# Self-attention key and value projections as seven quarter products in one go, with token sums on GpSimd and weight sums formed once

## The chip, the cores and the metric

The kernel runs on one core of a Trainium2 chip. The metric is the device time of one execution in microseconds (us). Engines: PE is TensorE (matmuls and transposes; its weight loads stand as PEld), DVE is VectorE, ACT is ScalarE, POOL is GpSimd, SP issues the DMAs.

## The reference

An encoder layer over a context of 77 tokens and a decoder layer over 2048 tokens, for two batches, width 512, 16 heads of 32, all in fp32. The part that matters is the decoder's causal self-attention:

```python
yn = _ln(y, dec_n1_s, dec_n1_b)
y = y + _mha(yn, yn, dec_sa_in_w, dec_sa_in_b, dec_sa_out_w, dec_sa_out_b, sb)
# in _mha, with xq = xkv = yn:
wq, wk, wv = jnp.split(w_in, 3, axis=0)
q = (xq @ wq.T + bq) ...;  k = (xkv @ wk.T + bk) ...;  v = (xkv @ wv.T + bv) ...
scores = jnp.einsum("bhqd,bhkd->bhqk", q, k) / sqrt(hd) + bias
attn = jax.nn.softmax(scores, axis=-1)
out = jnp.einsum("bhqk,bhkd->bhqd", attn, v)
```

After it come cross attention over the encoder's output and a feed-forward layer of width 2048.

## The kernel before

**Blocks and units.** The self-attention works through 8 blocks of 512 tokens, `(b, m)` for two batches and m = 0 to 3. A block has 16 units, one for each group of four heads (g) and each tile of 128 query tokens (t), so there are 128 units; u is the number of a block's first unit, x the block's number from 0. Because of the causal mask, a unit has m*4 + t + 1 chunks of 128 keys (1 to 16).

**What a unit does.** PE forms the scores of four heads (`scores`, L373), up to four chunks to a bank of PSUM. DVE copies them to SBUF and takes the maxima (L382, L389), then their negative maximum `nm` (L399). ACT forms four exponentials over the whole row, one per head (L404). PE transposes the probabilities (`turn`, L427), chunk by chunk with the four heads of each; half of the transposed tiles are copied from PSUM by ACT (L433) and half by DVE (L431). PE then multiplies by the values (`values`, L444). PSUM has 7 banks in a ring (`bank()`), taken by scores, transposes and projections alike.

**The order of the work** is fixed by hand. All engines' queues are filled by one program loop: transposes of up to eight chunks of unit n, then (after the last of them) `slot(n + 1)`, then the next scores, then the values of unit n, then more scores. A slot holds jobs written into dictionaries by slot number: `light` (ahead of the projections), `jobs` (projections) and `late`:

```python
def slot(n):
    for f in light[n]:
        f()
    for _, run, _ in jobs[n]:
        load_next()
        run(loaded[ran[0]])
        ran[0] += 1
    for f in late[n]:
        f()
```

Up to two of the later exponentials of unit n + 1 are queued on ACT during the transposes of unit n, the rest behind `slot(n + 1)`.

**Projections.** Each of `q_job` (L216), `k_job` (L227), `v_job` (L240) and `out_job` (L252) is four matmuls of 128x512 into one bank and one drain. Queries and keys are made by group of heads (weights of 256 KB into `wqk`, L200), values and outputs by tile of 128 tokens (weights of 1 MB into the one buffer `wbig`, L206). The drain of the keys is on ACT for m < 2 (L232) and on DVE otherwise (L230), that of the values on DVE (L243). The 16 jobs of a block lie in 16 slots, from u-5 to u+10: query u-5, u-1, u+3, u+5; keys u-4, u, u+4, u+6; values u-3, u-2, u+1, u+2 (for m = 0: u+1 to u+4; one slot later for the second block); outputs u+7 to u+10. So nearly each slot has one job. The first slots of all also have the encoder's stages (L544 to L634), and slots 65 to 94 a first part of the cross attention.

**GpSimd in the self-attention** has the power of the variance (L286), the norm's centring (L293), residual sums (L267), the division of the outputs (L472), the encoder's subtraction and division (L596, L608), and from the third block on differences of the feed-forward weights (line L1113).

**The seven products.** The feed-forward layer and the later cross attention already use Winograd's form for a product of 2x2 quarters: seven products (table `ONE`) with sums of quarters of the weights (S1 to S4) and of the tokens (T1 to T4), in place of eight. There a product of 128x256 matmuls runs at L1376, L1493 and L1536. The sums of weights are made once on GpSimd during the self-attention (`wc_sums`) and stored in DRAM.

Of the kernel before, what the change touches and what calls it, by code (L numbers as in the profile page):

```python
# [10 lines left out]
F32 = mybir.dt.float32  # L11
AF = mybir.ActivationFunctionType
ALU = mybir.AluOpType
# [41 lines left out]
def tile_encoder_decoder(ctx: ExitStack, tc: tile.TileContext, ins, out):  # L55
    nc = tc.nc
    x, src = ins["x"], ins["ctx_1024"]
# [8 lines left out]
    dram = ctx.enter_context(tc.tile_pool(name="dram", bufs=1, space=DRAM))  # L66
# [11 lines left out]
    def vec(name, i):  # L78
        c = _COL[name] + i
        return vecs[:, c : c + 1]  # L80
# [78 lines left out]
    with (  # L159
# [6 lines left out]
        kT = ac.tile([P, NC, T], F32, name="kT")  # L166
        vv = ac.tile([P, T // P, D], F32, name="vv")
# [27 lines left out]
        nTs, qTs, ots, sums_of = {}, {}, {}, {}  # L195
        wbig, xs, xr = {}, {}, {}
# [26 lines left out]
        def k_job(b, m, g):  # L223
            def run(w):
                mm = bank()
                for c in range(NC):
                    nc.tensor.matmul(mm, w[:, c, :], nTs[b, m][:, c, :], start=(c == 0), stop=(c == NC - 1))  # L227
                d, bi = kT[:, g, ts(m, MB)], vec("dec_sa_in_b", NC + g)
                if m >= 2:
                    nc.vector.tensor_scalar(d, mm, bi, None, ALU.add)  # L230
                else:
                    nc.scalar.activation(d, mm, AF.Identity, bias=bi)  # L232

            return lambda: small_w(D + g * P), run, True

        def v_job(b, m, t):
            def run(w):
                mm = bank()
                for c in range(NC):
                    nc.tensor.matmul(  # L240
                        mm, nTs[b, m][:, c, ts(t, P)], w[:, c, :], start=(c == 0), stop=(c == NC - 1)
                    )
# [168 lines left out]
        got = {}  # L411
# [515 lines left out]
            return plan  # L927


        blocks = [(b, m) for b in range(B) for m in range(NMB)]  # L930
        NU = NC * TB
        jobs = {n: [] for n in range(-1, len(units) + NU)}
        light = {n: [] for n in range(-1, len(units) + NU)}

        ahead = {n: [] for n in range(-1, len(units) + NU)}
        late = {n: [] for n in light}

        for x, (b, m) in enumerate(blocks):
            u = x * NU
            first = m == 0  # L940

            jobs[max(u - 5, -1)].append(q_job(b, m, 0))
# [52 lines left out]
        v = pp[:H, 13056 : 13056 + 3 * LT].rearrange("h (m u) -> h m u", u=LT)  # L995
# [96 lines left out]
        light[len(units) - 1].append(last_loads)  # L1092


        TOK = MB // 2
        gp, ve = nc.gpsimd, nc.vector


        w1_d = dram.tile([4, NC, P, D], F32, name="w1_d")
# [3 lines left out]
        free = pp[:, 3 * HC * MB : END - 3 * HC * MB]  # L1103
# [8 lines left out]
        def minus(engine, out, a, b):  # L1112
            engine.tensor_tensor(out, a, b, ALU.subtract)  # L1113

        def w2_sums(c):

# [49 lines left out]
        def quarter(name, r, c):  # L1166

            return ins[name][r * TOK : (r + 1) * TOK, c * TOK : (c + 1) * TOK].rearrange("(c p) o -> p c o", p=P)

        def wc_sums(name, turned):  # L1170
            z = free.rearrange("p (z k o) -> p z k o", z=8, k=2)
            q = {}
            for i, (r, c) in enumerate(((0, 0), (0, 1), (1, 0), (1, 1))):
                nc.sync.dma_start(z[:, i], quarter(name, c, r) if turned else quarter(name, r, c))
                q[r, c] = z[:, i]
            s1, s2, s3, s4 = (z[:, 4 + i] for i in range(4))
            if turned:
                gp.tensor_tensor(s1, q[1, 0], q[1, 1], ALU.add)
                minus(gp, s2, s1, q[0, 0])
                minus(gp, s3, q[0, 0], q[1, 0])  # L1180
                minus(gp, s4, q[0, 1], s2)
            else:
                minus(gp, s1, q[0, 1], q[0, 0])
                minus(gp, s3, q[1, 1], q[0, 1])
                minus(gp, s2, q[1, 1], s1)
                minus(gp, s4, q[1, 0], s2)

        def wc_store(dst):
            nc.sync.dma_start(
                dst.rearrange("s p x -> p s x"), free[:, 4 * D :].rearrange("p (s x) -> p s x", s=4)  # L1190
            )

        for u, name, turned, dst in (
            (2 * NU, "dec_ca_in_wT", True, wq_d), (6 * NU, "dec_ca_out_wT", False, wo_d)
        ):
            light[u + 7].append(lambda name=name, turned=turned: wc_sums(name, turned))
            late[u + 8].append(lambda dst=dst: wc_store(dst))
# [6 lines left out]
        u = 6 * NU  # L1204
        for n, k in enumerate((0, 2, 4, 10)):
# [5 lines left out]

        ONE = (
            ("11", "11", 0, True, "11"),
            ("12", "21", 1, True, "11"),
            ("S2", "T2", 0, False, "12"),
            ("S1", "T1", 1, True, "22"),
            ("S3", "T3", 0, False, "22"),
            ("S4", "22", 1, False, "12"),  # L1220
            ("22", "T4", 0, False, "21"),
        )
        TWO = (
            ("11", "11", 0, True, "11"),
            ("S1", "T1", 1, True, "22"),
# [67 lines left out]
        def of_n(name):  # L1293
# [5 lines left out]
        T_OF = {"T1": ("12", "11"), "T2": ("22", "T1"), "T3": ("22", "12"), "T4": ("21", "T2")}  # L1299

        def sum_n(name, of):
            minus(gp, of(name), *(of(a) for a in T_OF[name]))


        sets = [[high[:, (4 * a + k) * D : (4 * a + k + 1) * D] for k in range(4)] for a in range(2)]
# [59 lines left out]
        chains = [None]  # L1365
# [243 lines left out]
        i = 0  # L1609
        while i < len(stream):  # L1610
            n = stream[i][0]
# [91 lines left out]
```

## Time and profile before

| | |
|---|---|
| median of 3 runs | 2808.68 us (2805.91 to 2808.88) |
| profiled execution | 2804.72 us, span 2802.9 us |
| mean granted clock of TensorE | 0.995 |
| DMA | 355 MB, mean 127 GB/s |
| self-attention | from 28 us (first transposes of unit 0) to about 1726 us |

Groups stand as: line, engine, operation, out<-in, shape, count | busy us, mean ns of one | idle time before them and what ended it. Timelines stand as: start us, length us, engine, line, operation, operands, count [idle before <-releaser]. Matmuls are pipelined, so the length of one in a group mean is longer than its share of the busy time.

### The profile page before, as it was taken

The page shows a single profiled execution, that of the slowest core. Times are in us where ns is not written, and L with a number is a line of the kernel's source. Part 1 is how long each engine was busy: PE and PEld are TensorE (multiplying, and loading weights), DVE is VectorE, ACT ScalarE, POOL GpSimd, SP SyncE. Part 2 cuts the span into 40 slices and gives each one's busy share as a digit, 9 for nine tenths or more (in the row PEclk, how much of TensorE's full clock was granted, in tenths as well). Part 3 has the DMA queues.
Part 4 walks back from the last instruction along what each step waited for, and adds up shares of the span by engine and source line. Part 5 has one row for each costly group of instructions (what it writes and reads, how often), then busy time and mean ns, then how long its engine had stood idle before and what let it go on. Part 6 is the DMA issues. An engine that isn't in the chain of part 4 may idle for free. (4 is left out here: it accounts for less than half of the span.)

```text
span 2802.9 us, 65879 instructions
## 1 busy us (share of the span) xinstructions
PE 2769.8 (99%) x25998; PEld 2079.2 (74%) x25998; DVE 1858.9 (66%) x5360; ACT 1430.6 (51%) x2751; POOL 875.4 (31%) x745
## 2 busy tenths in 40 slices
PE   9899999999999999999999999999999999999998
PEld 5557666666666556666666677898989898989898
DVE  4666587778887567687778886464555655464645
ACT  3544466556666546656656676435343444444431
POOL 0301043300100302221200001374647474746456
PEclk9899999999999999999999999999999999999999
DMA  6414344411112512232310113574747574656475
GB/s 174 128 45 138 121 144 125 133 37 40 39 40 77 137 53 62 92 107 88 104 40 17 41 57 130 167 245 143 240 146 244 170 228 161 224 162 222 145 228 181
DMA packets 281270, 355.30 MB, mean 127 GB/s; under 512 B 37968, under 2 KB 156544, under 8 KB 280834
## 3 DMA queue, kind: packets, MB, share of 16 engines
q1 hardware_dynamic: 280962, 351.10, 40.3%
q8 instruction: 205, 3.36, 0.5%
q14 instruction: 103, 0.84, 0.1%
HBM read 309.51 MB, written 41.49 MB: 125 GB/s over the span
## 5 line engine op out<-in xcount | busy, mean ns | idle before, releaser
L404 ACT ACTIVATE pp<-pp,nm 128x128 f32<-128x128 f32 (+15 forms) x512 | 612.1, 1202 | 231.8 <-DVE nm L399 231.4
L382 DVE TENSOR_SCALAR_CACHE_REDUCE pp<-psum 128x512 f32<-128x512 f32 (+3 forms) x1024 | 559.4, 590 | 65.2 <-PE psum L373 63.4
L427 PEld LDWEIGHTS psum<-ident,pp 128*128 128x128 f32 x4352 | 472.4, 141 | 106.0 <-DVE pp L382 51.9
L427 PE MATMUL psum<-ident,pp 128*128 128x128 f32 x4352 | 533.2, 277 | 7.0 <-ACT pp L404 3.7
L433 ACT COPY pts<-psum 128x512 f32<-128x512 f32 (+3 forms) x592 | 297.0, 575 | 435.2 <-PE psum L427 305.4
L431 DVE COPY pts<-psum 128x512 f32<-128x512 f32 (+2 forms) x544 | 330.0, 659 | 66.0 <-PE psum L427 65.7
L373 PE MATMUL psum<-kT,q 32*128 32x512 f32 (+3 forms) x2560 | 357.1, 575 | 4.9 <-DVE pp L382 2.5
L444 PEld LDWEIGHTS psum<-pts,vv 128*32 128x32 f32 x8704 | 226.0, 110 | 124.4 <-issue 116.6
L1405 PE MATMUL psum<-pp 128*128 128x128 f32 x2560 | 304.5, 276 | 1.9 <-POOL pp L1113 1.6
L1405 PEld LDWEIGHTS psum<-pp 128*128 128x128 f32 x2560 | 296.3, 192 | 8.6 <-issue 2.8
L444 PE MATMUL psum<-pts,vv 128*32 128x128 f32 x8704 | 279.0, 275 | 0.7 <-ACT pts L433 0.5
L1113 POOL TENSOR_TENSOR pp<-pp 128x512 f32<-128x512 f32 x159 | 212.6, 1354 | 108.7 <-DMA pp<-in_dec_ff_wT_dram 49.7
L1376 PE MATMUL psum<-vv,pp 128*128 128x256 f32 x1024 | 236.2, 381 | 0.0
L373 PEld LDWEIGHTS psum<-kT,q 32*128 32x128 f32 x2560 | 123.8, 184 | 140.2 <-issue 91.3
L1376 PEld LDWEIGHTS psum<-vv,pp 128*128 128x128 f32 x1024 | 190.3, 190 | 25.8 <-issue 0.5
L389 DVE CUSTOM_DVE_ANT_0 pp<-psum,bias 128x256 f32<-128x256 f32 (+1 forms) x512 | 195.9, 411 | 16.7 <-PE psum L373 16.6
L1389 DVE TENSOR_TENSOR kT<-kT,psum 128x512 f32<-128x512 f32 x96 | 65.8, 686 | 190.0 <-PE psum L1376 189.8
L1376 PE MATMUL psum<-nT,pp 128*128 128x256 f32 x768 | 174.1, 380 | 0.0
L1392 ACT ACTIVATE kT<-kT,vecs 128x256 f32<-128x256 f32 x192 | 87.0, 501 | 156.7 <-DVE kT L1389 156.0
L286 POOL TENSOR_TENSOR rstd<-rstd,mhalf 128x1 f32<-128x1 f32 x32 | 18.5, 578 | 472.4 <-DVE rstd L285 450.9
L1376 PEld LDWEIGHTS psum<-nT,pp 128*128 128x128 f32 x768 | 144.2, 190 | 20.3 <-issue 1.6
L472 POOL TENSOR_TENSOR oT<-rirows,oT 128x512 f32<-128x512 f32 x30 | 38.6, 1287 | 357.3 <-DMA rirows<-rec 270.5
(207 smaller groups left out, 3792.7 us busy)
## 6 DMA issues: line engine op xcount, KB each, us to landing
pp<-w_d SPq DMA_DIRECT2D x520, 256.0 KB
pp<-in_dec_ff_wT_dram SPq DMA_DIRECT2D x112, 256.0 KB
wqk<-in_dec_sa_in_wT_dram SPq DMA_DIRECT2D x64, 256.0 KB
bias<-tzg SPq DMA_DIRECT2D x128, 128.0 KB
pp<-wo_d SPq DMA_DIRECT2D x56, 256.0 KB
wbig<-in_dec_sa_in_wT_dram SPq DMA_DIRECT2D x8, 1024.0 KB
vv<-in_enc_ff_wT_dram SPq DMA_DIRECT2D x8, 1024.0 KB
wbig<-in_dec_sa_out_wT_dram SPq DMA_DIRECT2D x8, 1024.0 KB
```

The source lines that it names most:

```text
L373: nc.tensor.matmul(banks[r][:, : kn * P], q[rows4(r), ts(t, P)], kT[rows4(r), g, k0 * P : (k0 + kn) * P], start=True, stop=True,)
L382: nc.vector.tensor_scalar(p[:, k0 * P : (k0 + far) * P], s[:, : far * P], 1.0, None, ALU.mult, ALU.max, accum_out=st["mx"][:, r, c : c + 1],)
L389: nc.vector.tensor_tensor_reduce(p[:, (i + 1) * P - w : (i + 1) * P], s[:, far * P : kn * P], biases[b, m, g][:, r, 2 * P - w :], 1.0, LOW ...
L404: nc.scalar.activation(p, p, AF.Exp, bias=nm, accum_out=to)
L427: nc.tensor.transpose(pt[:, ts(x, P)], state[n]["p"][r][:, ts(k, P)], ident)
L431: nc.vector.tensor_copy(pts[:, : len(load), :], pt[:, :w])
L433: nc.scalar.copy(pts[:, : len(load), :], pt[:, :w])
L444: nc.tensor.matmul(ot[rows4(r), t, :], vv[:, k, ts(g * HC + r, HD)], got.pop((n, k, r)), start=(k == 0), stop=(k == i),)
L1113: engine.tensor_tensor(out, a, b, ALU.subtract)
L1376: nc.tensor.matmul(mm[:, ts(f, TOK)], a[:, c, ts(f, P)], b[:, c, :], start=fresh and f == 0 and c == 0, stop=c == 1, skip_group_check=True,)
L1392: nc.scalar.activation(dst[:, e, :], src[:, e, :], AF.Relu, bias=vec("dec_ff1_b", f + e))
L1405: nc.tensor.matmul(psum[:, bank_i, ts(col, P)], lhs[:, c, :], w[:, c, :], start=fresh and k in (0, 3) and c == 0, stop=c == 3, skip_group_ ...
```

## The change

For keys, in the six blocks with m > 0 other than the first block of all, and for values, in seven blocks (all but the first), the four jobs of 4 matmuls are replaced by one job of seven products in one slot: keys in slot u-4, values in slot u+1. A product is four matmuls of 128x256 (two row tiles of 128, two chunks of the contraction). The products alternate between two banks; a bank is accumulated on while its earlier state is drained (`ONE`'s column `fresh`). Drains of keys: four on ACT (two instructions of 128x256 each) and three additions on DVE; of values: seven on DVE. In slot u-5 GpSimd forms four token sums of 128x512 into buffers of the tags `xt` and `xr`. The weight tiles (256 KB each, quarters of the weights or sums) come through `wbig`, now a ring of four, refilled after each product. The sums of the weights are made on GpSimd in slots 3 (keys) and 6 (values), in a part of `kT` that is not in use yet, and stored to DRAM in slots 4 and 7. Query jobs and output jobs stay where they were, so the slots u-3, u-2, u, u+2, u+4 and u+6 have no projection left. The functions `minus`, `sum_n`, `quarter`, `wc_sums` and the table `ONE` are moved up in the file; `wc_store` writes four DMAs in place of one.

```diff
+        def wc_sums(name, turned, z, c0=0):
+            z = [t.rearrange("p (k o) -> p k o", k=2) for t in z]
+            q = {}
+            for i, (r, c) in enumerate(((0, 0), (0, 1), (1, 0), (1, 1))):
+                nc.sync.dma_start(z[i], quarter(name, c, r, c0) if turned else quarter(name, r, c, c0))
+                q[r, c] = z[i]
+            s1, s2, s3, s4 = z[4:]
+            if turned:
+                gp.tensor_tensor(s1, q[1, 0], q[1, 1], ALU.add)
+                minus(gp, s2, s1, q[0, 0])
...
+        def wc_store(dst, z):
+            for i in range(4):
+                nc.sync.dma_start(dst[i], z[4 + i])
+        kv_ring = [wbt[:, i, :].rearrange("p (c o) -> p c o", c=2) for i in range(NC)]
...
+        def kv_feed():
+            while kv_fed[0] < min(len(kv_tiles), kv_used[0] + len(kv_ring)):
+                nc.sync.dma_start(kv_ring[kv_fed[0] % len(kv_ring)], kv_tiles[kv_fed[0]])
+                kv_fed[0] += 1
...
+        def token_sums(b, m, kinds):
+            n_tiles[b, m] = [
+                sb.tile([P, D], F32, name=tag, tag=tag, bufs=2) for tag in ("xt", "xt", "xr", "xr")
+            ]
+            for kind in kinds:
+                kv_want(kind)
+            kv_feed()
+            for name in ("T1", "T2", "T3", "T4"):
+                sum_n(name, lambda n: of_nT(b, m, n))
+
+        def products(kind, b, m):
+            chains = bank(), bank()
+            for j, (_, by, chain, fresh, to) in enumerate(ONE):
+                w, n, mm = kv_next(), of_nT(b, m, by), chains[chain]
+                for f in range(2):
+                    for c in range(2):
+                        left, right = (w, n) if kind == "k" else (n, w)
+                        nc.tensor.matmul(
+                            mm[:, ts(f, TOK)], left[:, c, ts(f, P)], right[:, c, :],
+                            start=fresh and f == 0 and c == 0, stop=c == 1, skip_group_check=True,
+                        )
+                kv_feed()
...
+                if to in [p[4] for p in ONE[:j]]:
+                    ve.tensor_tensor(d, got, d, ALU.add)
+                elif kind == "k":
+                    for f in range(2):
+                        nc.scalar.activation(
+                            d[:, f, :], got[:, f, :], AF.Identity, bias=vec("dec_sa_in_b", NC + 2 * r + f)
+                        )
+                else:
+                    ve.tensor_tensor(d, got, bv[:, None, ts(r, TOK)].to_broadcast([P, 2, TOK]), ALU.add)
...
-            jobs[max(u - 4, -1)].append(k_job(b, m, 0))
-            jobs[(u + 1 if first else u - 3 + (x == 1)) if x else -1].append(v_job(b, m, 0))
-            jobs[(u + 2 if first else u - 2 + (x == 1)) if x else 1].append(v_job(b, m, 1))
-            jobs[u + 3 if first else u + 1].append(v_job(b, m, 2))
-            jobs[u + 4 if first else u + 2].append(v_job(b, m, 3))
+            seven = ("k" if x and not first else "") + ("v" if x else "")
+            if seven:
+                light[u - 5].append(lambda b=b, m=m, kinds=seven: token_sums(b, m, kinds))
+            if "k" in seven:
+                jobs[u - 4].append(products_job("k", b, m))
+            else:
+                jobs[max(u - 4, -1)].append(k_job(b, m, 0))
+            if "v" in seven:
+                jobs[u + 1].append(products_job("v", b, m))
+            else:
+                for t, n in enumerate((-1, 1, 3, 4)):
+                    jobs[n].append(v_job(b, m, t))
             jobs[u - 1 if x else 0].append(q_job(b, m, 1))
-            jobs[u if x else 2].append(k_job(b, m, 1))
+            if "k" not in seven:
+                jobs[u if x else 2].append(k_job(b, m, 1))
             for g, at, then in ((2, 3, 4), (3, 5, 6)) if x else ((2, 3, 4), (3, 5, 6)):
                 jobs[u + at].append(q_job(b, m, g))
-                jobs[u + then].append(k_job(b, m, g))
+                if "k" not in seven:
+                    jobs[u + then].append(k_job(b, m, g))
...
+        spare = [kT[:, g, (2 + h) * MB : (3 + h) * MB] for g in range(NC) for h in range(2)]
+        for n, kind in ((3, "k"), (6, "v")):
+            light[n].append(lambda kind=kind: wc_sums("dec_sa_in_wT", True, spare, sa_from[kind]))
+            late[n + 1].append(lambda kind=kind: wc_store(sa_d[kind], spare))
```

More of the change, by code (lines that the diff above doesn't have):

```diff
@@ L927, in first_cross, with minus @@
             return plan
+        TOK = MB // 2
+        gp, ve = nc.gpsimd, nc.vector
+        def minus(engine, out, a, b):
+            engine.tensor_tensor(out, a, b, ALU.subtract)
+        ONE = (
+            ("11", "11", 0, True, "11"),
+            ("12", "21", 1, True, "11"),
+            ("S2", "T2", 0, False, "12"),
+            ("S1", "T1", 1, True, "22"),
+            ("S3", "T3", 0, False, "22"),
+            ("S4", "22", 1, False, "12"),
+            ("22", "T4", 0, False, "21"),
+        )
@@ new lines, in tile_encoder_decoder, with sum_n, quarter @@
+        T_OF = {"T1": ("12", "11"), "T2": ("22", "T1"), "T3": ("22", "12"), "T4": ("21", "T2")}
+        def sum_n(name, of):
+            minus(gp, of(name), *(of(a) for a in T_OF[name]))
+        def quarter(name, r, c, c0=0):
+            o = c0 + c * TOK
+            return ins[name][r * TOK : (r + 1) * TOK, o : o + TOK].rearrange("(c p) o -> p c o", p=P)
+        def wc_sums(name, turned, z, c0=0):
[8 more added lines that the diff above has]
+                minus(gp, s2, s1, q[0, 0])
+                minus(gp, s3, q[0, 0], q[1, 0])
+                minus(gp, s4, q[0, 1], s2)
+            else:
+                minus(gp, s1, q[0, 1], q[0, 0])
+                minus(gp, s3, q[1, 1], q[0, 1])
+                minus(gp, s2, q[1, 1], s1)
+                minus(gp, s4, q[1, 0], s2)
@@ new lines, in wc_store, with kv_want @@
+        def wc_store(dst, z):
+            for i in range(4):
+                nc.sync.dma_start(dst[i], z[4 + i])
+        sa_d = {k: dram.tile([4, P, D], F32, name=f"sa_{k}", tag=f"sa_{k}") for k in "kv"}
+        sa_from = {"k": D, "v": 2 * D}
+        kv_ring = [wbt[:, i, :].rearrange("p (c o) -> p c o", c=2) for i in range(NC)]
+        kv_tiles, kv_fed, kv_used, n_tiles = [], [0], [0], {}
+        def kv_want(kind):
+            for name, *_ in ONE:
+                if name[0] == "S":
+                    kv_tiles.append(sa_d[kind][int(name[1]) - 1].rearrange("p (c o) -> p c o", c=2))
+                else:
+                    kv_tiles.append(quarter("dec_sa_in_wT", int(name[1]) - 1, int(name[0]) - 1, sa_from[kind]))
@@ new lines, in kv_feed, with kv_next, of_nT @@
+        def kv_feed():
+            while kv_fed[0] < min(len(kv_tiles), kv_used[0] + len(kv_ring)):
+                nc.sync.dma_start(kv_ring[kv_fed[0] % len(kv_ring)], kv_tiles[kv_fed[0]])
+                kv_fed[0] += 1
+        def kv_next():
+            kv_used[0] += 1
+            assert kv_used[0] <= kv_fed[0]
+            return kv_ring[(kv_used[0] - 1) % len(kv_ring)]
+        def of_nT(b, m, name):
+            if name[0] == "T":
+                return n_tiles[b, m][int(name[1]) - 1].rearrange("p (c o) -> p c o", c=2)
+            r, c = int(name[0]) - 1, int(name[1]) - 1
+            return nTs[b, m][:, 2 * r : 2 * r + 2, ts(c, TOK)]
@@ L930, in tile_encoder_decoder, with products_job @@
+        def products_job(kind, b, m):
+            return lambda: None, lambda _: products(kind, b, m), False
         blocks = [(b, m) for b in range(B) for m in range(NMB)]
@@ L1110, in tile_encoder_decoder @@
         SUBS = ("11", "21", "T2", "T1", "T3", "22", "T4")
-        def minus(engine, out, a, b):
-            engine.tensor_tensor(out, a, b, ALU.subtract)
         def w2_sums(c):
@@ L1164, in w1_store @@
             )
[L1166 to L1191, printed above, removed]
         for u, name, turned, dst in (
@@ L1195, in tile_encoder_decoder @@
         ):
-            light[u + 7].append(lambda name=name, turned=turned: wc_sums(name, turned))
-            late[u + 8].append(lambda dst=dst: wc_store(dst))
+            z = free.rearrange("p (z x) -> p z x", z=8)
+            z = [z[:, i] for i in range(8)]
+            light[u + 7].append(lambda name=name, turned=turned, z=z: wc_sums(name, turned, z))
+            late[u + 8].append(lambda dst=dst, z=z: wc_store(dst, z))
         u = 2 * NU
@@ L1297, in of_n @@
             return nTt[:, 2 * r : 2 * r + 2, ts(c, TOK)]
-        T_OF = {"T1": ("12", "11"), "T2": ("22", "T1"), "T3": ("22", "12"), "T4": ("21", "T2")}
-        def sum_n(name, of):
-            minus(gp, of(name), *(of(a) for a in T_OF[name]))
         sets = [[high[:, (4 * a + k) * D : (4 * a + k + 1) * D] for k in range(4)] for a in range(2)]
```

20 lines of the change are left out of this document (9 added, 11 removed).

## The prediction, made before the changed kernel had run

> **What bounds the kernel now.** I read the page's busy shares first, then the groups by line and form for the prices of matmuls, then the timelines of PE, ACT and DVE beside each other around single units, because the change moves work between slots.
>
> ```profile
> PE 2769.8 (99%) x25998; PEld 2079.2 (74%) x25998; DVE 1858.9 (66%) x5360; ACT 1430.6 (51%) x2751; POOL 875.4 (31%) x745
> ```
>
> PE is busy 99% of the span, so the time is the sum of its matmuls plus the little that it waits. Every slot of the attention has some projection in it, and that projection covers the time in which VectorE takes the maxima and ScalarE the exponentials of the next unit. The change makes the projections cheaper, and it also takes them out of most slots. Both effects have to be priced.
>
> **The work removed.** A fp32 matmul is two instructions in the trace.
>
> ```profile
> L1389 DVE TENSOR_TENSOR kT<-kT,psum 128x512 f32<-128x512 f32 x96 | 65.8, 686 | 190.0 <-PE psum L1376 189.8
> L1376 PE MATMUL psum<-nT,pp 128*128 128x256 f32 x768 | 174.1, 380 | 0.0
> L1392 ACT ACTIVATE kT<-kT,vecs 128x256 f32<-128x256 f32 x192 | 87.0, 501 | 156.7 <-DVE kT L1389 156.0
> ```
>
> ```profile
> L240 PE MATMUL psum<-wbig,nT 128*128 128x512 f32 x256 | 116.4, 597 | 0.1
> L227 PE MATMUL psum<-nT,wqk 128*128 128x512 f32 x256 | 116.0, 596 | 0.1
> ```
>
> L227 is all key projections of 8 blocks and L240 all value projections: 116.0/8 = 14.5 us and 116.4/8 = 14.6 us for one projection of a block. The new form has 7 products of 4 matmuls with 256 columns, 56 instructions; L1376 does the same shape in the feed-forward layer at 174.1/768 = 0.227 us, so 12.7 us. The keys change in 6 blocks and the values in 7: 13 x 1.8 = **-23.5 us** of PE.
>
> **The slots emptied.** Before, a block's 8 key and value pieces of 3.6 us lay in 8 different slots. After, the keys stand in one slot (u-4) and the values in one (u+1), and the slots u-3, u-2, u, u+2, u+4 and u+6 have nothing (u is the block's first unit). That is 36 slots in six blocks, and three in the first block of the second batch, which lose one piece each. The question for each is whether the unit's transposes, which follow, could start 3.6 us earlier. Unit 34 has 11 chunks (block 2, slot u+2); its PE rows, its exponentials and the copy before them:
>
> ```profile
> 406.02 1.09 PE L427 MATMUL psum<-ident,pp 128*128 128x128 f32 x8
> 406.95 3.60 PE L240 MATMUL psum<-wbig,nT 128*128 128x512 f32 x8
> 410.48 1.14 PE L373 MATMUL psum<-kT,q 32*128 32x512 f32 x8
> 411.55 0.64 PE L444 MATMUL psum<-pts,vv 128*32 128x128 f32 x16
> 412.12 3.71 PE L427 MATMUL psum<-ident,pp 128*128 128x128 f32 x32
> ```
>
> ```profile
> 404.05 1.47 ACT L404 ACTIVATE pp<-pp,nm 128x1408 f32<-128x1408 f32 x1 [4.64 <-DVE nm L399]
> ...
> 410.15 1.46 ACT L404 ACTIVATE pp<-pp,nm 128x1408 f32<-128x1408 f32 x1
> ```
>
> ```profile
> 409.11 0.69 DVE L431 COPY pts<-psum 128x512 f32<-128x512 f32 x1
> ```
>
> The first exponential waited for VectorE's maximum, and the fourth ends at 410.15 + 1.46 = 411.6 us. The fourth transpose of a chunk needs it; it ran at about 412.4 (412.12 and three transposes). Nothing in this chain waits for the piece at 406.95, so without it PE arrives 3.5 us earlier, at 408.9, and stands: first for the copy that ends at 409.8, then for the exponential. The transposes move from 412.4 to 411.7 only. Of the 3.5 us that leave the slot 2.8 stay as a wait. Units of 11 chunks meet an empty slot three times per batch (u+2 and u+6 of block 2, u-2 of block 3), so 6 x 2.8 = **+16.8 us**. The first unit of a block with m = 3, 13 chunks, is worse:
>
> ```profile
> 610.11 3.60 PE L227 MATMUL psum<-nT,wqk 128*128 128x512 f32 x8
> ...
> 615.72 0.55 PE L427 MATMUL psum<-ident,pp 128*128 128x128 f32 x3
> 617.50 3.38 PE L427 MATMUL psum<-ident,pp 128*128 128x128 f32 x29 [1.24 <-ACT pp L404]
> ```
>
> ```profile
> 610.68 1.68 ACT L404 ACTIVATE pp<-pp,nm 128x1664 f32<-128x1664 f32 x1 [0.56 <-DVE nm L399]
> ...
> 615.69 1.67 ACT L404 ACTIVATE pp<-pp,nm 128x1664 f32<-128x1664 f32 x1
> ```
>
> PE already waits 1.24 us here for the last exponential (615.69 + 1.67 = 617.4), which runs back to back from 610.68. Removing the key piece at 610.11 removes nothing: 2 x 3.5 = **+7 us**. The counter-example is unit 36 with 9 chunks (u+4):
>
> ```profile
> 434.29 1.97 PE L427 MATMUL psum<-ident,pp 128*128 128x128 f32 x16
> 436.09 3.60 PE L227 MATMUL psum<-nT,wqk 128*128 128x512 f32 x8
> ...
> 441.27 3.27 PE L427 MATMUL psum<-ident,pp 128*128 128x128 f32 x28
> ```
>
> ```profile
> 432.58 1.26 ACT L404 ACTIVATE pp<-pp,nm 128x1152 f32<-128x1152 f32 x1
> ```
>
> Its exponentials end at 433.8, 7 us before the transposes, so the 3.6 us come out whole. The other 31 slots lie between these two: bounds 0 and 3.5 us each. Most units with 9, 13 (not first), and 15 chunks resemble unit 36; the units with 2 to 7 chunks are nearer to unit 34, with a part of the piece left as a wait. I take a tenth of a piece on average, 0.35 us: 31 x 0.35 = **+11 us** (0 to 30).
>
> **The clock.** The traces show what PE pays beyond a wait itself:
>
> ```profile
> 97.25 1.20 PE L585 MATMUL psum<-pp 32*77 32x77 f32 x26 [3.16 <-ACT pts L433]
> ...
> 101.19 3.62 PE L427 MATMUL psum<-ident,pp 128*128 128x128 f32 x16
> ...
> 111.91 1.65 PE L373 MATMUL psum<-kT,q 32*128 32x384 f32 x4 [2.08 <-ACT pts L433]
> ```
>
> ```profile
> 97.30:105.00 7.70, 7.52 (x80) 6.55 (x80) 5.75 (x19) 5.18 (x16) 5.78 (x5) 0.52 0.01 3
> ```
>
> After an idle time of 3.16 us the granted clock was 0.52 for the next 7.7 us, and 16 transposes took 3.62 us where the same 16 take 1.97 at 434.29. After 1.24 us (617.50) it did not drop: 29 transposes in 3.38 us. The eight large waits are 2.8 us in two parts, and 4.8 us (1.24 + 3.5). Bounds: nothing, or half of 7.7 us each time, 8 x 3.9 = 31 us. The lost work is partly hidden in waits that exist anyway, so I take 2 us each, **+16 us**. The Trainium skill, page "TensorE: Matmul & The Clock Gate", section "What's actually happening", puts the drop to half clock after at least one idle window of about 3.4 us; by that rule this term would be 2 x 2 = 4 us in place of 16, since only the waits of 4.8 us are as long. The row at 97.25 has its drop after 3.16 us, a little below that figure, so the measurement decides; the rule's case is the first rival below.
>
> **Smaller terms.** Weight sums: two sets of four loads and four POOL sums in slots 3 and 6. POOL is idle near slot 3. In slot 6 the sums of the value weights stand in POOL's order behind the first and ahead of the second of these:
>
> ```profile
> 86.09 2.07 POOL L293 TENSOR_SCALAR xt<-xt,bnmv,rstd 128x512 f32<-128x512 f32 x1
> 91.08 2.25 POOL L596 TENSOR_TENSOR pp<-pp,emx 77x1232 f32<-77x1232 f32 x1 [2.92 <-DVE emx L595]
> ```
>
> ```profile
> 345.88 2.04 SPq L1121 DMA_DIRECT2D pp<-in_dec_ff_wT_dram  x4
> ```
>
> ```profile
> 352.59 3.85 POOL L1113 TENSOR_TENSOR pp<-pp 128x512 f32<-128x512 f32 x3 [0.28 <-DMA pp<-in_dec_ff_wT_dram]
> ```
>
> Four tiles issued from 345.88 were there at 352.59, 6.7 us later, and three sums take 3.85 us, so four 5.1. Loads issued at about 86 let the sums run from 92.5 to 97.7, and L596, with the encoder's softmax and the norms of the next block, comes 6.7 us late. POOL's own idle time and ScalarE's work take up most; **+1.5 us** (0 to 7). The stores of the sums wait on SP's queue; the loads behind them wait for their buffers until later anyway.
>
> Token sums: four per block, 5.1 us on a POOL that is 31% busy, one slot ahead of their use: nothing, and up to 5 us a block where POOL is late.
>
> Within the seven products: a chain's bank is drained before the next but one product writes it. PE needs 12.7/7 = 1.8 us for one product, and the drain is 0.69 us on DVE (L1389) or two of 0.50 us on ACT (L1392): hidden, while DVE and ACT have no queue ahead. Exponentials behind the key drains on ACT's queue come late in the slot after; **+1 us** in all. The ring of four weight tiles is refilled by SP when a product ends, with three products (5.4 us) until it is needed; of the four tiles of 345.88 to 347.9 the last, issued at about 347.4, was there at 352.59, 5.2 us with three others ahead of it, so one alone takes less: nothing. If each refill came 1 us late, 13 us.
>
> **Sum.** -23.5 + 16.8 + 7 + 11 + 16 + 1.5 + 1 = **+29.8 us**. The profiled execution took 2804.72 us (span 2802.9), 4 us under the median of 2808.68. On the profiled execution's time the sum gives 2834.5, on the median 2838.5; I forecast **2838 us**. About 0.2%, 5.6 us, is what a measurement of this kernel can tell from no change.
>
> **Rivals.** First, the clock holds: waits as above, but those of 2.8 us, split in two, do not lower it, and perhaps not even the two of 4.8 us. For it: 1.24 us did not lower it, and the waits have parts of about that length. Against it: both parts fall into one stretch of about 3 us. The time is 2838 - 16 = 2822 us, or 2826 if the two longest pay. Second, the other side: the waits are not there, because the maxima of the next unit come earlier once DVE has no drain of a piece in an empty slot and has caught up in the long slot before. For it: DVE would lose its 0.69 us in each empty slot. Against it: in unit 34 that drain stood behind the maximum that counts, and its chain began after the neighbour's transposes, which the long slot does not move. It decides if the eight large waits shrink below 1 us and the others vanish: -23.5 + 8 + 2.5 = -13 us, 2796 us. Third, the refills are late: SP waits in order for each product, and what it issues queues behind other loads. At 1 us for each of the 13 sets and as much again in lowered clock: 2838 + 26 = 2864 us; SP's rows above show issues well ahead, against it.
>
> **Chances.** Forecast 0.50, clock holds 0.24, waits absorbed 0.17, refills late 0.09. The range takes in the case of the clock (2822, and below it the other slots at their lower bound of 0, 2811) and the forecast with its terms for the clock and other slots higher by 20 us: 2808 to 2858. What it leaves out is most of the faster case and the latest refills. Faster by over 0.2%: 0.17. Within 0.2%: 0.07, the lower end of the second case. Slower: 0.76.
>
> **What would show it.** The page has PE's own waits for exponentials now:
>
> ```profile
> L427 PE MATMUL psum<-ident,pp 128*128 128x128 f32 x4352 | 533.2, 277 | 7.0 <-ACT pp L404 3.7
> ```
>
> Right: these 3.7 us grow to over 15; slices of PE with 8 in blocks 2, 3, 6 and 7; a granted clock under 1.00 between 400 and 720 us; the new matmul line at 0.227 us an instruction. PE's idle time among the encoder's stages, 90 to 120 us, tells of the POOL term. Wrong: transposes of 11-chunk units starting within 12 us of the unit before, or PE's idle time unchanged with its busy time down by 23 us; or PE waiting for a DMA inside the products.

## The result and the profile after

The changed kernel takes 2857.32 us (median of 4, 2853.07 to 2860.2) against 2807.3 us for the kernel before on the same chip: a ratio of 1.0178, 95% interval 1.0160 to 1.0196. It is slower by 50 us, at the upper edge of the predicted range. The profiled execution took 2860.2 us (before 2804.72), 55.5 us more; the account below is made against that.

The page of the changed kernel, engines' busy times, two of its slice rows, the group of the transposes and that of the score matmuls:

```profile
PE 2793.9 (98%) x26310; PEld 2164.8 (76%) x26310; DVE 1871.8 (65%) x5383; ACT 1447.0 (51%) x2791; POOL 920.9 (32%) x781
...
PE   9899999999999999999999999999999999999998
...
PEclk9899999999999999999999999999999999999999
...
L427 PE MATMUL psum<-ident,pp 128*128 128x128 f32 x4352 | 546.5, 280 | 18.1 <-ACT pp L404 14.8
L373 PE MATMUL psum<-kT,q 32*128 32x512 f32 (+3 forms) x2560 | 383.4, 579 | 7.3 <-ACT pts L433 4.3
```

The last of these groups on the page of the kernel before:

```profile
L373 PE MATMUL psum<-kT,q 32*128 32x512 f32 (+3 forms) x2560 | 357.1, 575 | 4.9 <-DVE pp L382 2.5
```

PE waits 14.8 us for exponentials (L404) where it waited 3.7. But PE's busy time has grown by 24 us, although its products have become cheaper: the score matmuls (L373), as many as before, are busy for 26.3 us more, the transposes for 13.3 us more. The slots of unit 34, the unit on which the prediction argued, show why; PE's rows, then ScalarE's:

```profile
424.16 1.09 PE L427 MATMUL psum<-ident,pp 128*128 128x128 f32 x8
425.18 2.71 PE L373 MATMUL psum<-kT,q 32*128 32x512 f32 x8
427.82 0.64 PE L444 MATMUL psum<-pts,vv 128*32 128x128 f32 x16
428.40 0.55 PE L427 MATMUL psum<-ident,pp 128*128 128x128 f32 x3
429.89 3.38 PE L427 MATMUL psum<-ident,pp 128*128 128x128 f32 x29 [0.95 <-ACT pp L404]
```

```profile
425.38 1.47 ACT L404 ACTIVATE pp<-pp,nm 128x1408 f32<-128x1408 f32 x1
...
428.30 1.46 ACT L404 ACTIVATE pp<-pp,nm 128x1408 f32<-128x1408 f32 x1
```

The value piece (3.60 us) between the first two rows is gone. The fourth exponential ends at 429.76 and the fourth transpose follows at 429.89, as predicted. Only 0.95 us of the wait stands as idle time; another part is inside the eight score matmuls, which took 1.14 us before and 2.71 us now. PE's weight loads show what these wait for:

```profile
426.16 0.29 PEld L373 LDWEIGHTS psum<-kT,q 32*128 32x128 f32 x2 [0.32 <-DVE pp L382]
426.77 0.29 PEld L373 LDWEIGHTS psum<-kT,q 32*128 32x128 f32 x2 [0.32 <-DVE pp L382]
```

They are released one matmul at a time, 0.61 us apart, by VectorE's maxima (L382), which also take the earlier scores out of PSUM. In PE's own rows these waits count as busy. The page's slices therefore show 9 where I expected 8.

### The profile page after: what moved, and what is told of

The parts are those of the page before. It is cut to its first block, busy times and chain, and to the rows that moved or that the text cites. A ratio compares the mean times of both kernels' runs of the same rounds, so it can differ in the third digit from the quotient of the medians.

```text
span 2858.3 us, 66873 instructions
## 1 busy us (share of the span) xinstructions
PE 2793.9 (98%) x26310; PEld 2164.8 (76%) x26310; DVE 1871.8 (65%) x5383; ACT 1447.0 (51%) x2791; POOL 920.9 (32%) x781
## 5 line engine op out<-in xcount | busy, mean ns | idle before, releaser
L404 ACT ACTIVATE pp<-pp,nm 128x128 f32<-128x128 f32 (+15 forms) x512 | 612.1, 1202 | 230.7 <-DVE nm L399 230.4
L382 DVE TENSOR_SCALAR_CACHE_REDUCE pp<-psum 128x512 f32<-128x512 f32 (+3 forms) x1024 | 558.7, 590 | 55.0 <-PE psum L373 53.6
L427 PEld LDWEIGHTS psum<-ident,pp 128*128 128x128 f32 x4352 | 479.5, 142 | 123.2 <-DVE pp L382 52.6
L427 PE MATMUL psum<-ident,pp 128*128 128x128 f32 x4352 | 546.5, 280 | 18.1 <-ACT pp L404 14.8
L373 PE MATMUL psum<-kT,q 32*128 32x512 f32 (+3 forms) x2560 | 383.4, 579 | 7.3 <-ACT pts L433 4.3
L431 DVE COPY pts<-psum 128x512 f32<-128x512 f32 (+2 forms) x544 | 330.4, 659 | 83.7 <-PE psum L427 83.1
L373 PEld LDWEIGHTS psum<-kT,q 32*128 32x128 f32 x2560 | 136.5, 184 | 131.6 <-issue 77.4
```

What stands on the lines that cost most here:

```text
L373: nc.tensor.matmul(banks[r][:, : kn * P], q[rows4(r), ts(t, P)], kT[rows4(r), g, k0 * P : (k0 + kn) * P], start=True, stop=True,)
L382: nc.vector.tensor_scalar(p[:, k0 * P : (k0 + far) * P], s[:, : far * P], 1.0, None, ALU.mult, ALU.max, accum_out=st["mx"][:, r, c : c + 1],)
L404: nc.scalar.activation(p, p, AF.Exp, bias=nm, accum_out=to)
L427: nc.tensor.transpose(pt[:, ts(x, P)], state[n]["p"][r][:, ts(k, P)], ident)
L431: nc.vector.tensor_copy(pts[:, : len(load), :], pt[:, :w])
```

## The account by slots

I compared when each unit's transposes start in the two traces. A slot that lost one old piece should be 3.53 us shorter, and one that took seven products (12.18 us) for a piece 8.65 us longer; what it falls short of that is a loss (a wait in the middle of a unit's transposes shows in the slot behind). The first row is 13 x (12.18 - 4 x 3.53), the others sum such losses; the fifth is what the others leave.

| term | predicted, us | in the traces, us |
|---|---|---|
| 13 sets of seven products for four pieces | -23.5 | -25.2 |
| six 11-chunk units in empty slots, with the slot behind | +16.8 | +17.0 |
| clock at these six | +12 | 0 |
| first unit of the two blocks with m = 3, clock included | +7 and +4 | +11.3 |
| the other emptied slots and their neighbours | +11 (0 to 30) | +34.3 |
| POOL's weight sums (units 7 to 10) | +1.5 | +7.2 |
| weight refill in slot 65 | 0 | +9.0 |
| start of the run | - | +1.8 |
| exponentials behind key drains | +1 | in the others |
| sum | +29.8 | +55.4 |

## Experiments

Theory 1: the time is lost where slots were emptied, since PE needs cover there for the next unit's maxima and exponentials. Rival, theory 2: the seven products themselves cost it, by sums on POOL, late weights and three more drains a set. All ratios below are to the kernel before.

**Old products, new places.** First attempt, then one in which each load into the large tile waits its turn.

```
-            jobs[max(u - 4, -1)].append(k_job(b, m, 0))
...
+                for g in range(NC):
+                    jobs[u - 4].append(k_job(b, m, g, True))
...
+            for t, n in enumerate((-1, 1, 3, 4)):
+                jobs[u + 1 if x else n].append(v_job(b, m, t))
```

> The kernel before, with its old products (four pieces of 3.6 us for the keys, four for the values) but put where the change puts them: the four key pieces of a block in slot u-4, the four value pieces in slot u+1, in the same blocks. No seven products, no token sums, no weight sums, no ring of quarters; the key weights come in one load into the large weight tile. Theory 1, the emptied slots cost the time: the traces of before and after give 82 us of loss over what the products save, of which 7 lie where POOL's weight sums stand, 9 in slot 65 with its wait for a load and 2 at the start, so about 64 are the slots: 2807 + 64 = 2871 us (2855 to 2880), and PE waits for exponentials (transposes, by ACT L404) of over 15 us. Theory 2, the products themselves cost it (sums on POOL, weights late, additions on DVE): no more than 8 us from the kernel before, 2800 to 2815.

2918.58 us, 1.0400 (1.0386 to 1.0415). The load of the key weights into the large tile was issued ahead of output projections that still read it; these used the key weights, and PE waited 35.1 us in 6 waits for that load. So the run settles nothing. With the order of the loads mended:

> As the first clumped kernel, the old products with the four key pieces of a block in slot u-4 and the four value pieces in slot u+1, but each load into the large weight tile is issued only when all pieces that read the tile before have been issued (there the load of the key weights overtook the output projections, which read wrong weights and waited for them). The drains are those of the kernel before: four for each set, not seven. Theory 1, the emptied slots cost the time: 2871 us (2855 to 2880). Theory 2, the products themselves cost it (sums on POOL, weights late, more drains on VectorE): 2800 to 2815. Between the two if both share it: then what the changed kernel loses beyond this one, after its saving of 26 us, is the products' part.

2873.98 us, 1.0243 (1.0228 to 1.0258), against 2871 by theory 1. Without one of the seven products, one sum on POOL or one more drain, the loss is there, and in the same slots: by the account above the 11-chunk units cost 18.6 us (17.0 in the changed kernel), the first units of the two blocks 11.6 (11.3) and the other emptied slots 31.7 (34.3). PE's waits, summed, in this kernel (L438 is L427 of the others, L415 is L404):

```profile
PE psum L438 <- ACT pp L415: 14.9, 17, 1.3
PE psum L384 <- ACT pts L444: 6.4, 5, 2.1
PE psum L263 <- DMA wbig<-in_dec_sa_out_wT_dram: 5.5, 1, 5.5
```

14.9 us for exponentials against 14.8 in the changed kernel. Around unit 34 it stands as there, row for row:

```profile
425.19 2.71 PE L384 MATMUL psum<-kT,q 32*128 32x512 f32 x8
...
429.91 3.38 PE L438 MATMUL psum<-ident,pp 128*128 128x128 f32 x29 [0.95 <-ACT pp L415]
```

The two also give the products' own price. One set of values in block 2, first product to next scores; the changed kernel, then this one:

```profile
400.98 3.62 PE L1023 MATMUL psum<-wbig,nT 128*128 128x256 f32 x16
...
413.16 1.14 PE L373 MATMUL psum<-kT,q 32*128 32x512 f32 x8
```

```profile
399.35 13.04 PE L251 MATMUL psum<-wbig,nT 128*128 128x512 f32 x30
...
413.18 1.14 PE L384 MATMUL psum<-kT,q 32*128 32x512 f32 x8
```

12.18 us for seven products, 13.83 for four pieces that stand together: 1.65 us less. Each in a slot of its own, as in the kernel before, the four take 14.12 us, 1.94 us more than the seven products, and 13 x 1.94 = 25.2 us. (The 5.5 us for the output weights above come from this kernel's own order of loads.)

**POOL's sums earlier.**

```
-        for n, kind in ((3, "k"), (6, "v")):
-            light[n].append(lambda kind=kind: wc_sums("dec_sa_in_wT", True, spare, sa_from[kind]))
...
+        light[4].append(lambda: wc_store(sa_d["k"], spare))
+        light[4].append(lambda: wc_sums("dec_sa_in_wT", True, spare, sa_from["v"]))
```

> The changed kernel with the sums of the value weights moved from slot 6 to slot 4, where POOL has nothing to do; otherwise as it is. Theory 1, POOL's four sums in slot 6 delay the encoder's softmax (L596 from 91.1 to 102.6) and through it units 7 to 10, 7.2 us with what the clock loses: 2857 - 7 = 2850 us, ratio 1.015 to the kernel before, PE's idle of 3.40 us before L305 at 107 us gone. Theory 2, my prediction's term of 1.5 us was right and the 7 us come from something else in this stretch: 2855 to 2857, and L596 still after 100 us.

2853.75 us, 1.0165 (1.0151 to 1.0179), 3.6 us less than the changed kernel, whose interval it overlaps: between the 2850 of theory 1 and the 2855 of theory 2. The traces decide for theory 1. POOL in the changed kernel, then here:

```profile
97.60 1.27 POOL L963 TENSOR_TENSOR kT<-kT 128x512 f32<-128x512 f32 x1 [7.70 <-DMA kT<-in_dec_sa_in_wT_dram]
98.95 3.73 POOL L934 TENSOR_TENSOR kT<-kT 128x512 f32<-128x512 f32 x3
102.64 2.25 POOL L596 TENSOR_TENSOR pp<-pp,emx 77x1232 f32<-77x1232 f32 x1
```

```profile
91.11 2.25 POOL L596 TENSOR_TENSOR pp<-pp,emx 77x1232 f32<-77x1232 f32 x1 [2.97 <-DVE emx L595]
```

In the changed kernel POOL stands 7.70 us in front of the sums for their weights' loads, and the softmax product behind them starts at 102.64. Here it starts at 91.11, and units 7 to 10 are together 5.3 us shorter. The medians differ by 3.6 us, less than that. In this run's trace the wait in slot 65 grew from 7.8 to 10.8 us, as its sum of waits shows; whether it did so in the other executions is not known:

```profile
PE psum L1023 <- DMA wbig<-sa_v: 10.8, 2, 9.8
```

**The refills of slot 65.**

```
-            light[len(units) // 2 + 1 + r] += fs
+            (light if r else late)[len(units) // 2 + 1 + r] += fs
```

> The changed kernel with the loads of the first cross attention (ten issues on SP from 918.5 us) put behind the value products of slot 65 instead of in front of them; otherwise as it is. Theory 1, the weight refills of slot 65 were late because they stood behind these loads on SP's queue and shared the DMA engines with them: the wait of 7.13 us inside the products goes, with 2 us of lowered clock: 2857 - 9 = 2848 us. Theory 2, a refill into the ring takes too long wherever it is issued: the wait stays at over 3 us, 2853 to 2857.

2848.44 us, 1.0148 (1.0134 to 1.0162); theory 1 said 2848. The wait in the changed kernel, PE and then SP's queue:

```profile
922.01 3.62 PE L1023 MATMUL psum<-wbig,xt 128*128 128x256 f32 x16
932.77 3.61 PE L1023 MATMUL psum<-wbig,xr 128*128 128x256 f32 x8 [7.13 <-DMA wbig<-sa_v]
```

```profile
918.52 1.79 SPq L887 DMA_DIRECT2D pp<-y  x4
...
924.41 2.73 SPq L992 DMA_DIRECT2D wbig<-sa_v  x2
```

The first product ended near 920.4, yet its refill was issued at 924.41, behind the cross attention's loads, and the tile was there at 932.7. With those loads behind the products this product follows at once (slot 65 is 9.0 us shorter). The second product row shows eight matmuls in 3.61 us where 16 take 3.62 above it: half clock after the wait.

**The seven products, spread.** If slots need cover, the same products in the old slots should save the time. The set has to be cut where its running sum can be put by.

```
-                jobs[u - 4].append(products_job("k", b, m))
...
-                jobs[u + 1].append(products_job("v", b, m))
...
+        ORDER = ("11", "12", "S2"), ("S1", "S4"), ("S3", "22")
...
+                places = ("k", 0, -4), ("k", 1, -2), ("v", 0, 0), ("k", 2, 1), ("v", 1, 2), ("v", 2, 5)
```

> The same seven products for the same blocks, in three parts each (three, two and two products) spread over the slots: keys in u-4, u-2 and u+1, values in u, u+2 and u+5, the query piece of u+5 in u+6; the first block of the second batch has its values in u+1, u+2 and u+4. Slots u-3 and u+4 (u+3 in that block) stay empty. The running sum of the first chain is put by between parts, which adds one addition on POOL for each set of keys and two for each set of values. Weight sums and token sums as in the change. Theory 1, the emptied slots cost the time: of the 82 us over the products' saving 7 (POOL's weight sums) stay and perhaps 10 in the slots still empty, so 2807 - 26 + 17 = 2798 us (2788 to 2812). Theory 2, the products themselves cost it: 2845 to 2860.

2870.51 us, 1.0226 (1.0212 to 1.0240), a miss for both numbers. The last value part read its ring tiles after the output weights had been loaded over them (so these products used the wrong weights), and PE waited 20.2 us for that load. Mended, with the two fixes from above:

> The seven products in three parts over the slots as in the first spread kernel, with three places mended: the last part of the values reads its two weight tiles from the small weight buffers, so that it no longer stands behind the load of the output weights in the large tile; the sums of the value weights are formed in slot 4; the loads of the first cross attention stand behind the value products of slot 65. Theory 1, the emptied slots alone cost the time: 2807 - 26 + about 9 for the slots still empty = 2790 us (2780 to 2800). Theory 3, seven drains for four cost it too, since VectorE takes 0.69 us for each just when the next maxima are due: the slots with two products in place of one piece were 1.1 to 1.9 us longer in the first spread kernel though PE's work there differs by 0.1 us; taking from its 61 us the 38 of the last value parts, 7 of slot 65 and 4 of POOL leaves 12, so 2819 us (2810 to 2827).

2834.02 us, 1.0091 (1.0075 to 1.0108): neither 2790 nor quite 2819. So I tried the drains:

```
-                ve.tensor_tensor(dest(to), got, dest(other or to), ALU.add)
...
+                nc.scalar.copy(d, got)
...
+                gp.tensor_tensor(dest(to), got, other, ALU.add)
```

> The spread kernel with the mended places, and its additions taken from VectorE: ScalarE copies a product from PSUM into a tile that is free, and POOL adds it (only the fourth product of S4 of the keys stays on VectorE). POOL has some five more operations of 1.3 us for a set of seven. Theory 3, drains on VectorE delay the next maxima: the slots with two products lose their 1.1 to 1.9 us, about 20 us in all, 2799 us (2790 to 2810). Theory 1, they do not matter: as the kernel beside it, within 5 us. A rival: the copies on ScalarE delay the exponentials as much as VectorE's drains did the maxima: as the kernel beside it or slower.

2841.96 us, 1.0130 (1.0115 to 1.0145), slower than with the drains on VectorE. Most of its slots with two products still were 1.0 to 2.2 us longer than before, though VectorE has fewer drains. This alone does not rule theory 3 out, since the copies may cost as much on ScalarE: PE's waits for exponentials rose from 1.4 to 5.8 us. PE's rows in slot 34, the kernel with VectorE's drains and then this one, show what it was:

```profile
417.68 1.99 PE L1060 MATMUL psum<-wbig,xt 128*128 128x256 f32 x8 [0.30 <-DVE pp L382]
420.71 1.99 PE L1060 MATMUL psum<-wbig,nT 128*128 128x256 f32 x8 [1.04 <-DVE vv L1076]
```

```profile
414.06 1.99 PE L1060 MATMUL psum<-wbig,xt 128*128 128x256 f32 x8 [0.30 <-DVE pp L382]
417.42 1.99 PE L1060 MATMUL psum<-wbig,nT 128*128 128x256 f32 x8 [1.37 <-ACT vv L1077]
```

The second product of a part accumulates on the first one's bank, so PE stands until that is drained: 1.04 us behind VectorE, 1.37 behind ScalarE, whose copy starts at 416.80, when its exponentials end. In the changed kernel the two chains alternate and hide it; my cut put two products of one chain side by side.

```
-                add("22", product("S1", 1, True), "21")
-                add("12", product("S4", 1, False))
+                got = product("S1", 0, True)
+                add("22", got, "21")
+                add("12", got)
+                add("12", product("S4", 1, True))
```

> As the mended spread kernel with its additions on VectorE, but in the parts of two products (S1 and S4, S3 and 22) each product has a PSUM bank of its own, where the second was accumulated on the first before; so the first is added to two quarters by VectorE, one addition of 0.69 us more for each part of two, 26 in all. Theory 4, the parts of two lose their time because the second product writes to the bank of the first and PE stands until that is drained: the 25 waits of 0.78 to 2.58 us between the two, 25 us in sum without the one for a weight tile, go, so 2834 - 25 = 2809 us (2798 to 2814), at or a little over the kernel before. Theory 3, VectorE's drains delay the next maxima: with 26 more of them it gets slower, 2840 or more.

2803.78 us, 0.9988 (0.9979 to 0.9997): 30 us faster, with 26 drains more on VectorE. Theory 4 holds and theory 3 falls. Slot 34 now, and the largest wait left inside the products, in this kernel's sum of waits:

```profile
410.15 1.89 PE L1057 MATMUL psum<-wbig,xt 128*128 128x256 f32 x8
411.88 1.89 PE L1057 MATMUL psum<-wbig,nT 128*128 128x256 f32 x8
```

```profile
PE psum L1057 <- DMA wqk<-in_dec_sa_in_wT_dram: 2.4, 1, 2.4
```

The last step takes that one away: S3 comes through the ring again, ahead of the output weights.

```
-                for name in ORDER[2]:
-                    jobs[u + 5].append(last_job(b, m, name))
+                jobs[u + 5].append((lambda: None, lambda _, b=b, m=m: products("v", b, m, 2, None, "S3"), False))
+                jobs[u + 5].append(last_job(b, m, "22"))
```

> As the spread kernel with a bank for each product, but of the last value part only the second tile comes through the small weight buffers; the first (S3) comes through the ring, ahead of the output weights' load. By the theory that holds so far (a slot costs what its unit lacks as cover, and a part of products must wait for neither a bank nor a tile) the waits for these tiles go, 2.37, 1.44 and 1.09 us in blocks 1, 5 and 4 with what follows them: 2804 - 5 = 2799 us (2794 to 2803), faster than the kernel before. If the tiles' loads are not what PE waits for there: 2802 to 2806.

**2794.42 us, 0.9958 (0.9944 to 0.9971)**, faster than both kernels. The page's lines for it:

```profile
PE 2760.7 (99%) x26310; PEld 2146.2 (77%) x26310; DVE 1895.5 (68%) x5422; ACT 1436.0 (51%) x2767; POOL 944.7 (34%) x801
...
L427 PE MATMUL psum<-ident,pp 128*128 128x128 f32 x4352 | 535.9, 278 | 4.6 <-ACT pp L404 1.4
```

The same 26310 matmuls as in the changed kernel, PE 33 us less busy and 1.4 us of waits for exponentials instead of 14.8. About half of the 25 us that the products save is left as gain. The time is 4.6 us better than I expected; by the traces some of the further gain lies in slots 77 and 78 and in the first unit of block 7, and I did not look for its cause.

**Other places for whole sets.**

```
-                jobs[u - 4].append(products_job("k", b, m))
+                jobs[u - (2 if m == 3 else 4)].append(products_job("k", b, m))
...
-                jobs[u + 1].append(products_job("v", b, m))
+                jobs[u + (m != 3)].append(products_job("v", b, m))
```

> The changed kernel with the value weights' sums in slot 4, the cross attention's loads behind the products of slot 65 (both as tried before, together about 2845 us), and in the two blocks with m = 3 the seven key products in slot u-2 instead of u-4 and the seven value products in slot u instead of u+1. Theory 1, a slot loses what its unit's exponentials need as cover: the waits of the first unit of these blocks (11 us for the two) and of the 11-chunk unit ahead of them (2.84 us each) go, and the slots that are emptied for it, of 9 and 14 chunks, lose 1.5 us or less each: 2845 - 14 = 2831 us (2826 to 2836). Rival: the waits go to the neighbouring slots, 2841 to 2849.

2835.64 us, 1.0104 (1.0090 to 1.0118), about 9 us under the sum of the two fixes (2857.3 - 3.6 - 8.9 = 2844.8, which was not run as one kernel). The time lies in theory 1's range, at its upper end, but by slots only 3.4 us in block 3 and 1.8 in block 7 come from the places, where theory 1 set 14. The three waits of the first unit went, 6.9 us in block 3. The 11-chunk unit gained 1.6 of its 2.84 us, and the slot emptied for it lost as much. And slot u+1 was the empty one now, and its unit, of 14 chunks, stood in the first one's place:

```profile
656.43 0.33 PE L427 MATMUL psum<-ident,pp 128*128 128x128 f32 x1 [0.85 <-ACT pp L404]
658.20 4.85 PE L427 MATMUL psum<-ident,pp 128*128 128x128 f32 x29 [1.44 <-ACT pp L404]
```

That cost 4.0 us. The rival is half right: a wait moves along with the empty slot, and a list of chunk counts is not enough to place work by. Why this unit stands where the one of slot u+2 does not in the changed kernel was not tried.

## Why the prediction was right in sign and 19 us short

**Products.** Right: -25.2 for -23.5. The forecast took the pieces' busy time, 14.5 us, and 12.7 us for seven; in place they are 14.12 and 12.18.

**Eight large waits.** The size was right, 17.0 us for 16.8 at the 11-chunk units, and so was what ends the wait. On the way there PE stands for VectorE, as forecast, though first for its maxima and only then for the copy that the forecast named. The first unit of the m = 3 blocks:

```profile
631.78 0.33 PE L427 MATMUL psum<-ident,pp 128*128 128x128 f32 x1
633.39 0.33 PE L427 MATMUL psum<-ident,pp 128*128 128x128 f32 x1 [1.28 <-ACT pp L404]
635.05 0.33 PE L427 MATMUL psum<-ident,pp 128*128 128x128 f32 x1 [1.34 <-ACT pp L404]
636.72 6.22 PE L427 MATMUL psum<-ident,pp 128*128 128x128 f32 x29 [1.34 <-ACT pp L404]
```

The idle sum, 3.96 us against 1.24 before, plus 2.84 us of lowered clock (29 transposes in 6.22 us for 3.38) makes 5.6 of this block's 6.4 us. L427's wait came to 14.8 us where I asked for over 15.

**The clock.** This step failed in its size: 16 us set, about 4 paid, and only at the two first units. The windows of 11-chunk unit 34 and behind the rows above, with the granted clock ahead of the last two columns:

```profile
405.00:440.00 35.00, 34.05 (x343) 24.51 (x342) 27.22 (x90) 17.52 (x26) 15.18 (x13) 1.00 0.86 255
...
636.00:643.00 7.00, 6.28 (x33) 6.12 (x37) 2.03 (x3) 3.01 (x6) 0.00 (x0) 0.53 0.34 93
```

At all six 11-chunk units the clock held at 1.00, as the first rival had it. The rule of the Trainium skill ("TensorE: Matmul & The Clock Gate", "What's actually happening": half clock after an idle window of about 3.4 us) gave the prediction an estimate of 4 us for this term, which is what was paid. Its threshold does not fit as a single wait, though: the row at 636.72 follows waits of 1.28, 1.34 and 1.34 us with a transpose between each, none near 3.4.

**The other emptied slots.** This is the step that cost the forecast: 11 us set, 34 paid, over its upper bound of 30. I took a tenth of a piece for each, from unit 36, and asked only whether the exponentials were done in time. Even unit 36 does not give its 3.6 us whole. Its score matmuls in the emptied slot, before and then after:

```profile
439.62 0.71 PE L373 MATMUL psum<-kT,q 32*128 32x256 f32 x8
```

```profile
453.63 1.47 PE L373 MATMUL psum<-kT,q 32*128 32x256 f32 x8
454.41 0.30 PEld L373 LDWEIGHTS psum<-kT,q 32*128 32x128 f32 x4 [0.32 <-DVE pp L382]
```

The exponentials end well ahead, as predicted, but PE now waits for VectorE to take earlier scores out of PSUM, and with the slot behind about 1.5 us of the 3.53 are lost. About 20 of the 34 us lie in slots 66 to 95, under units of 1 to 8 chunks, beside the first cross attention. In slot 66, which lost 4.7 us, the scores wait for ScalarE's copy of transposed tiles:

```profile
946.06 1.82 PE L373 MATMUL psum<-kT,q 32*128 32x512 f32 x2 [1.87 <-ACT pts L433]
```

The clumped old products lose time there too (4.9 us in slot 66, 3.3 in 77 and 3.1 in 78, where the changed kernel loses 4.7, 2.6 and 1.7), so it is the empty slot and not the products.

**POOL.** Mis-sized, 1.5 for 7.2 us, of which 5.3 went with the sums moved: the loads took POOL's place as well as the sums, and I let its idle time absorb both. The price lay at the range's end of 7.

**Refills.** I put them at nothing, and in 12 sets of 13 that was near enough: of 7.8 us that PE waits for these tiles 7.13 are one wait. In slot 65 the third rival happened, by what was said for it: SP queued other loads ahead.

**Rivals.** "The clock holds" was right on the clock, and its time was too low for the reasons above. "Waits absorbed" fell: at unit 34 the first exponential starts 7.38 us behind the first transpose of the unit before in both kernels (404.05 - 396.67 and 422.19 - 414.81), so the maxima came no earlier, and the waits stood. Taking the clock's error out, the forecast would have been 12 us lower; three terms that I had made small hid it: 34 - 11, 7.2 - 1.5 and 9.0. That the range still held the result, by 0.7 us, is partly luck: errors of opposite sign cancelled in part.

## What to carry to other kernels

Ahead of merging small work into one large piece, list which units the small pieces covered and how long each waits without them, for the copies that free its PSUM banks as well as for its exponentials; price the short units too, since the loss is paid per slot and the saving once. When a chain of accumulating products is cut, see which two products then follow each other on one PSUM bank. And read busy time with care: here PE's grew by 24 us while its work shrank.

## What the runs showed that I had not expected

Waits of 1.28, 1.34 and 1.34 us with 0.33 us of work between them were followed by a clock of 0.53 over the next 7 us, while 0.95 us behind stretched scores was not (1.00). A product on a bank that VectorE has still to drain waits 1.04 us, though the drain itself takes 0.68: it stands behind a copy (L431) that VectorE starts at 419.37. Eight score matmuls are recorded as one run of 2.71 us where they need 1.14; the idle time shows only in the rows of PE's weight loads.
